# Two small products ahead of the attention-times-values step, another order of a turn's steps, and other PSUM banks

## The chip, the cores and the metric

The kernel runs on one core of one Trainium2 chip. The metric is device microseconds of one execution, lower is better. The profile names the engines PE (TensorE: matmul; PEld is its weight load), DVE (VectorE), ACT (ScalarE), POOL (GpSimd) and SP (SyncE, which here issues nearly all DMAs). All data is float32, apart from the attention mask and the identity that adds it.

## The reference

The input is x, 16 sequences of 256 tokens of 128 features. It is layer-normalised first. The result is `x + s * silu(f)`: `s` is one selective state-space block, `f` is a transformer of six layers, and both read the same normalised x.

```python
# s: the state-space block
xs, z = split(xn @ W_in)                       # 128 + 128 channels
xs, z = silu(conv4(xs)), silu(conv4(z))        # depthwise, 4 taps
dt_low, Bc, Cc = split(xs @ W_xdbl)            # 64, 16, 16
delta = softplus(dt_low @ W_dt + 2 * inv_dt)
h[n] = exp(-(n + 1) * delta) * h[n] + delta * xs * Bc[n]   # over 256 tokens, 16 states n
s = concat(sum_n h[n] * Cc[n] + xs * D, z) @ W_out + b_out

# f: six times
t = shift_tokens(f)                            # second half of the features moved by one token
q, k, v = split(t @ Wqkv)                      # 16 heads of 64
q, k = rotary(l2norm(q) * qs), rotary(l2norm(k) * ks)
# each window of 32 queries sees its own 32 keys and those of the window before
f = f + softmax(8 * q k^T + mask) v @ Wo
t = layernorm(shift_tokens(f)) * g + b
f = f + (a * gelu(gate)) @ W2 + b2             # a, gate = split(t @ W1 + b1), 341 each
```

## The kernel before

The work of the transformer is cut into blocks of 128 tokens: two blocks per sequence, 32 per layer, 192 in six layers. A program loop runs over turns n from -4 to 192. In each turn every step of the tuple `order` is called once, for a block that lies a fixed number ahead of n: `(project, 4, 0)` multiplies block n + 4 by the q weights, `(score, 1)` computes scores of block n + 1, `(attend, 0)` multiplies block n's weights by v. So five blocks are in work at once. The scheduler is set to manual, so the order in which the tuple calls the steps is the order in which each engine's queue holds the instructions; an engine runs its own queue strictly in that order, and engines wait for each other by semaphores.

What the steps issue, for one block (each file line is the one that the profile shows):

| Step | Engine and line | What |
|---|---|---|
| `project` (i = 0 q, 1 k), `values` | PE L427 | 128 tokens by 1024 columns, four passes of 512 columns |
| `square` | ACT L438 | squares for the lengths, read from PSUM |
| `rotate`, `rotate2` | DVE L448, L459 | the two rotary products, read from PSUM |
| `add` | POOL L470 | sum of the two rotary products |
| `hand_out` | ACT L480, SP L491 to L494 | v copied out of PSUM, then 8 or 10 DMAs that lay it out by window in `v2` |
| `lengths`, `guess` | DVE L504, L515 to L519 | sums of squares, first guess of the inverse roots for two blocks |
| `refine`, `scale` | POOL L525 to L535, L542 | two iterations on the guess; q or k times it |
| `turn` and `turned_q`, `turned_k` | PE L552, ACT L556 | eight transposes, then the copy out of PSUM |
| `score` | PE L587, L601 | mask by a product with the identity, then 64 small products |
| `greatest`, `subtract`, `soften` | DVE L614, L624, ACT L633 | maximum, subtraction, exponential |
| `turn_weights`, `turned_weights` | PE L552, ACT L556 | eight transposes of the weights, the copy into `aT` |
| `attend` | PE L657 | 64 products of 64 by 32 by 65 columns; the 65th column of v holds ones, so it gives the sum |
| `divide_last`, `divide` | DVE L673, ACT L674; DVE L680, L681 | division by that sum, last head pair apart |
| `turn_out`, `turned_out` | PE L552, ACT L556 | eight transposes of the output, the copy into `oT` |
| `close`, `residual` | PE L708, DVE L718 | output product for two blocks at a time (every second turn), sum with x |

Small shapes in `attend` and `score` use tiles of 64 rows by 32 columns of the array, eight at a time. Each fp32 product is two passes in the profile, so 64 products show as 128 matmuls.

Two other threads of work are woven in. `feed` advances a generator of the feed-forward part (PE L326, L181, L349, L372; ACT L330, L173, L338, L357; DVE L154, L155, L360, L375), one per four blocks, three steps a turn. The state-space block runs over eight groups of 512 tokens, 18 turns each, during about the first five of the six layers: `prepare` makes the inputs (convolution on DVE, L220 and L227, read from PSUM), and per turn `bring` (SP L270) loads one state's rows, `decay` (ACT L296) makes the exponential, `drive` (POOL L301) the input, `advance` (DVE L288) runs the scan instruction along the tokens, `weigh` (POOL L281, L282) adds the state's part to y; `put_out` ends a group. `norms_on` does the first layer normalisation of later groups in the early turns. In the last layer, `end` closes a group at the end of a turn (ACT L395 with silu, DVE L397, PE L401, DVE L402).

PSUM has eight banks of 512 float32 columns, held as one tensor. The dictionary `where` gives each role its bank; `pair(name)` takes two banks from there on, `bank(name)` one. Two roles in one bank can't be alive at once: a product that writes a bank waits until the last reader of the earlier contents is through. `at`, `aT`, `o`, `qT` are single buffers, `sq` and the scan's tensors have two, `bc` three.

Of the kernel before, what the change touches and what calls it, by code (L numbers as in the profile page):

```python
# [18 lines left out]
H, DH, W = 16, 64, 32  # L19
# [11 lines left out]
def tile_kernel(ctx: ExitStack, tc: tile.TileContext, a, out):  # L31
    nc = tc.nc
# [8 lines left out]
    pst = ctx.enter_context(tc.tile_pool(name="pst", bufs=1, space=PSUM))  # L41


    where = dict(q="6", k="0", v="4", qT="4", kT="0", s="2", w="4", av="2", o="2", h0="6", h1="0", h2="4", e="7", l="6", pw="4", f="7", n="1")
    psum = pst.tile([128, 8, G], FP, name="psum")

    def pair(name):
        i = int(where[name])
        return psum[:, i : i + 2, :].rearrange("p b x -> p (b x)")

    def bank(name):
        return psum[:, int(where[name]), :]
# [591 lines left out]
    def attend(n):  # L644

        b = blocks[n]
        aT, v2 = b["aT"], v2s[b["blk"]]

        b["pav"] = pair("av").rearrange("p (r x) -> p r x", r=2)[:, :, 0 : 7 * VW]
        b["pav"] = b["pav"].rearrange("p r (c d) -> p r c d", c=7)  # L650
        b["pav7"] = [bank("e"), bank("l")]
        for c in (7, 0, 1, 2, 3, 4, 5, 6):
            for j in range(4):
                jj = slice(j * W, (j + 1) * W)
                for r in range(2):
                    rr = slice(r * 64, (r + 1) * 64)
                    nc.tensor.matmul(  # L657
                        b["pav7"][r][jj, 0:VW] if c == 7 else b["pav"][jj, r, c, :],
                        aT[rr, c, jj],
                        v2[rr, j, c * VW : (c + 1) * VW],  # L660
                        start=True,
                        stop=True,
                    )
# [87 lines left out]
    def feed():  # L751
# [5 lines left out]


    order = (
        (norms_on, None),  # L760
        (lengths, 3, 1),
        (guess, 3),
        (close, -1, 1),
        (residual, -1),
        (feed, None),
        (project, 4, 0),
        (prepare, None),
        (score, 1),
        (rotate, 4, 0),
        (turn_weights, 0),  # L770
        (rotate2, 4, 0),
        (greatest, 1),
        (state, None, weigh),
        (refine, 3),
        (subtract, 1),
        (scale, 2, 0),
        (turned_weights, 0),
        (project, 4, 1),
        (square, 4, 0),
        (state, None, bring),  # L780
        (values, 1),
        (scale, 2, 1),
        (add, 4, 0),
        (rotate, 4, 1),
        (state, None, decay),
        (hand_out, 1),
        (rotate2, 4, 1),
        (add, 4, 1),
        (attend, 0),
        (divide_last, 0),  # L790
        (state, None, drive),
        (turn, 2, 0),
        (divide, 0),
        (state, None, advance),
        (square, 4, 1),
        (lengths, 4, 0),
        (turned_q, 2),
        (feed, None),
        (feed, None),
        (state, None, put_out),  # L800
        (turn_out, 0),
        (turned_out, 0),
        (turn, 2, 1),
        (turned_k, 2),
        (close, 0, 0),
        (soften, 1),
    )
    last = DEPTH * BL - 1
    with tc.manual_schedule():
# [124 lines left out]
```

## Time and profile before

| What | Value |
|---|---|
| Median of 3 runs | 3447.9 us (3443.46 to 3448.29) |
| Profiled execution | 3446.38 us, span 3444.6 us, mean granted TensorE clock 0.988 |
| Busy PE / PEld | 3238.9 us (94%) / 2163.4 us (63%) |
| Busy DVE / ACT / POOL | 2810.2 us (82%) / 2123.3 us (62%) / 2598.0 us (75%) |
| L427 q, k and v products on PE | 1070.3 us, 2304 passes, mean 600 ns |
| L657 attend on PE | 332.8 us, 24576 passes |
| L288 scan on DVE | 277.3 us, 128 instructions, mean 2166 ns |
| Copies of v, issued by SP | 1152 of 130 KB, 2.4 us from issue to landing; 576 of 65 KB, 2.5 us |

Times in the profile are microseconds unless marked ns. A row of the timeline reads: start, length, engine, line, operation, output from input with shapes, count, and in brackets the idle time just before with what ended it. Matmuls overlap in the array, so a group's busy time is longer than its start-to-start step; sums over a queue are made from steps. PE is 90% busy or more in nearly every fortieth of the span; only the first and the last are clearly below. The weight loads of PE run beside its products.

### The profile page before, as it was taken

What the parts mean: (1) busy time and instruction counts of PE and PEld (TensorE: products, weight loads), DVE (VectorE), ACT (ScalarE), POOL (GpSimd) and SP (SyncE); (2) the same over time, 40 slices, a digit from 0 to 9 for tenths busy, and PEclk for the clock granted to TensorE, in tenths of its full rate; (3) what the DMA queues carried; (4) which work ended last, traced back from release to release, by engine and by line L of the source; (5) the groups of instructions that cost most, each with busy time, mean ns of one, the idle gap of its engine ahead of it and who ended that gap; (6) DMA issues with size and microseconds to landing.
All of it is one profiled execution on the core that took longest, in us unless ns stands there. A gap on an engine that the chain in (4) does not pass through costs nothing.

```text
span 3444.6 us, 139812 instructions
## 1 busy us (share of the span) xinstructions
PE 3238.9 (94%) x62080; PEld 2163.4 (63%) x62080; DVE 2810.2 (82%) x3705; ACT 2123.3 (62%) x2725; POOL 2598.0 (75%) x2358
## 2 busy tenths in 40 slices
PE   6999999999999999999999999999999999999986
PEld 3666666666666666666666666666666666666663
DVE  6898879887898789878987889788879987777663
ACT  4666657655666566656665666576666665666554
POOL 6688868986898589968996789688878996565550
PEclk9999999999999999999999999999999999999998
DMA  3433334433333334333333333334333432222222
GB/s 87 104 98 105 84 84 104 104 81 83 97 97 90 91 94 97 91 85 88 107 92 91 88 96 92 89 99 98 91 81 93 105 94 70 69 64 70 63 64 57
DMA packets 190680, 304.49 MB, mean 88 GB/s; under 512 B 32702, under 2 KB 56572, under 8 KB 190076
## 3 DMA queue, kind: packets, MB, share of 16 engines
q1 hardware_dynamic: 189788, 295.22, 33.9%
q8 instruction: 488, 8.00, 1.0%
q14 instruction: 116, 0.95, 0.1%
q10 hardware_dynamic: 288, 0.33, 0.0%
HBM read 94.81 MB, written 8.91 MB: 30 GB/s over the span
## 4 chain that ended last, share of the span: by engine, by line
PE 73%; DVE 12%; ACT 6%; POOL 5%; issue 4%; DMA 0%; SPq 0%; DVEq 0%; ACTq 0%; POOLq 0%
PE psum L427 23%; PE psum L552 14%; PE psum L708 9%; PE psum L657 7%; PE psum L349 7%; PE psum L601 6%; PE psum L372 3%; ACT oT L556 3%; DVE t L459 2%; DVE o L681 2%; PE psum L587 2%; DVE hs L288 1%; DVE t L448 1%; POOL t L470 1%; DVE cv L227 1%
## 5 line engine op out<-in xcount | busy, mean ns | idle before, releaser
L470 POOL TENSOR_TENSOR t<-t,t 128x1024 f32<-128x1024 f32 x384 | 957.1, 2502 | 355.0 <-DVE t L459 184.4
L427 PE MATMUL psum<-wqkv,xT 128*128 128x512 f32 x2304 | 1070.3, 600 | 18.6 <-DVE cv L227 7.2
L542 POOL TENSOR_TENSOR t<-t,y 128x1024 f32<-128x1024 f32 x384 | 723.1, 1905 | 7.5
L427 PEld LDWEIGHTS psum<-wqkv,xT 128*128 128x128 f32 x2304 | 417.4, 192 | 406.0 <-issue 304.5
L448 DVE TENSOR_TENSOR t<-psum,tab 128x1024 f32<-128x1024 f32 x384 | 467.9, 1219 | 143.9 <-PE psum L427 131.1
L556 ACT COPY aT<-psum 128x1024 f32<-128x1024 f32 x192 | 194.2, 1012 | 589.6 <-PE psum L552 589.6
L459 DVE TENSOR_TENSOR t<-psum,tab 128x1024 f32<-128x1024 f32 x384 | 465.9, 1213 | 0.0
L504 DVE TENSOR_REDUCE ss<-sq 128x16 f32<-128x1024 f32 x384 | 456.4, 1198 | 1.3
L552 PE MATMUL psum<-ident,t 128*128 128x128 f32 x3072 | 412.7, 277 | 20.8 <-POOL t L542 8.9
L438 ACT ACTIVATE sq<-psum 128x1024 f32<-128x1024 f32 x384 | 395.0, 1029 | 51.4 <-DVE t L459 51.0
L657 PEld LDWEIGHTS psum<-v,aT 64*32 64x32 f32 x24576 | 294.0, 105 | 200.9 <-issue 121.9
L708 PE MATMUL psum<-oT,wo 128*128 128x256 f32 x1536 | 357.5, 386 | 24.2 <-ACT oT L556 24.2
L657 PE MATMUL psum<-v,aT 64*32 64x65 f32 x24576 | 332.8, 227 | 47.0 <-issue 24.6
L552 PEld LDWEIGHTS psum<-ident,t 128*128 128x128 f32 x3072 | 340.4, 142 | 40.3 <-POOL t L542 11.7
L708 PEld LDWEIGHTS psum<-oT,wo 128*128 128x128 f32 x1536 | 283.8, 190 | 81.4 <-ACT oT L556 46.5
L480 ACT COPY vt<-psum 128x1024 f32<-128x1024 f32 x192 | 196.2, 1022 | 189.6 <-PE psum L427 189.6
L601 PEld LDWEIGHTS psum<-kT,qT 64*32 64x32 f32 x24576 | 282.8, 105 | 11.2 <-issue 0.8
L601 PE MATMUL psum<-kT,qT 64*32 64x64 f32 x24576 | 286.2, 226 | 0.0
L288 DVE TENSOR_TENSOR_SCAN hs<-dA,bc 128x512 f32<-128x512 f32 x128 | 277.3, 2166 | 0.0
L556 ACT COPY oT<-psum 128x1024 f32<-128x1024 f32 x192 | 194.8, 1014 | 124.9 <-PE psum L552 123.0
L349 PE MATMUL psum<-xn,w 128*128 128x512 f32 (+1 forms) x576 | 260.2, 601 | 6.0 <-ACT o L674 4.8
L624 DVE TENSOR_TENSOR at<-psum,top 128x1024 f32<-128x1024 f32 x192 | 235.1, 1225 | 25.3
(102 smaller groups left out, 4583.0 us busy)
## 6 DMA issues: line engine op xcount, KB each, us to landing
v<-vt SPq DMA_DIRECT2D x1152, 130.0 KB, 2.4
bc<-rows SPq DMA_DIRECT2D x128, 512.0 KB, 5.1
v<-vt SPq DMA_DIRECT2D x576, 65.0 KB, 2.5
wqkv<-in_Wqkv SPq DMA_DIRECT2D x18, 512.0 KB, 4.0
wo<-in_Wo SPq DMA_DIRECT2D x6, 512.0 KB, 4.0
first<-in_x SPq DMA_DIRECT2D x8, 256.0 KB, 5.0
xn<-xT SPq DMA_DIRECT2D x16, 128.0 KB, 2.4
pad<-xn SPq DMA_DIRECT2D x8, 256.0 KB
```

The lines of the kernel that those rows point to most:

```text
L349: nc.tensor.matmul(ph[0:n, i * G : (i + 1) * G], w1[:, i * DI + c0 : i * DI + c0 + n], xn, start=True, stop=True,)
L427: nc.tensor.matmul(pq[:, cc], xb, wq[:, cc], start=True, stop=True)
L448: nc.vector.tensor_tensor(t1.rearrange("p (h d) -> p h d", h=H), b["pq", i].rearrange("p (h d) -> p h d", h=H), table(n, i, 0).unsqueeze(1 ...
L459: nc.vector.tensor_tensor(t2.rearrange("p (h f d) -> p h f d", h=H, f=2), b["pq", i].rearrange("p (h f d) -> p h f d", h=H, f=2)[:, :, ::- ...
L470: nc.gpsimd.tensor_tensor(b["qk", i], b["qk", i], b["t2", i], ALU.add)
L504: nc.vector.tensor_reduce(b["ss"][:, j * H : (j + 1) * H], b["sq", i].rearrange("p (h d) -> p h d", h=H), AX.X, ALU.add,)
L542: nc.gpsimd.tensor_tensor(t3, t3, b["inv"][:, j * H : (j + 1) * H].unsqueeze(2).to_broadcast([128, H, DH]), ALU.mult,)
L552: nc.tensor.transpose(pt[:, cc], of[:, cc], ident)
L556: nc.scalar.copy(to, pt.rearrange("p (c t) -> p c t", c=NP))
L601: nc.tensor.matmul(sc4[jj, r, c, :], qT[rr, c, jj], kT[rr, c, k0 : k0 + 64], start=False, stop=True, skip_group_check=True,)
L657: nc.tensor.matmul(b["pav7"][r][jj, 0:VW] if c == 7 else b["pav"][jj, r, c, :], aT[rr, c, jj], v2[rr, j, c * VW : (c + 1) * VW], start=Tru ...
L708: nc.tensor.matmul(b["pw"][:, 0:L], wo[:, c, :], b["oT"][:, c, :], start=(c == 0), stop=(c == NP - 1), skip_group_check=True,)
```

## The change

Three edits, shown whole below. In `attend`, two products of 32 by 4 columns (one for each half of the rows) are put ahead of the others. They read the first 32 columns of the last head pair's `aT` and one column of each of the four window pieces of `v2`, and write a corner of the two last-head banks, which the products after them write again. The table `where` gives most roles other banks; in particular the last head pair (`e`, `l`) moves to banks 3 and 2, which scores and v also use, and the roles n and f move. And `order` lists the same steps, each as often and for the same block as before, in another order. In short, by PE: before, a turn goes output product, q, scores, turned weights, k, v, attend, turned q, turned output, turned k; after, it goes output product, turned weights, scores, q, k, attend, v, turned output, turned k, turned q.

```diff
--- before.py
+++ after.py
@@ -41,7 +41,7 @@
     pst = ctx.enter_context(tc.tile_pool(name="pst", bufs=1, space=PSUM))
 
 
-    where = dict(q="6", k="0", v="4", qT="4", kT="0", s="2", w="4", av="2", o="2", h0="6", h1="0", h2="4", e="7", l="6", pw="4", f="7", n="1")
+    where = dict(q="6", k="0", v="2", qT="6", kT="2", s="2", w="0", av="4", o="4", h0="6", h1="4", h2="0", e="3", l="2", pw="4", f="6", n="5")
     psum = pst.tile([128, 8, G], FP, name="psum")
 
     def pair(name):
@@ -649,6 +649,12 @@
         b["pav"] = pair("av").rearrange("p (r x) -> p r x", r=2)[:, :, 0 : 7 * VW]
         b["pav"] = b["pav"].rearrange("p r (c d) -> p r c d", c=7)
         b["pav7"] = [bank("e"), bank("l")]
+
+        for r in range(2):
+            rr = slice(r * 64, (r + 1) * 64)
+            nc.tensor.matmul(
+                b["pav7"][r][0:W, 0:4], aT[rr, 7, 0:W], v2[rr, :, 0], start=True, stop=True
+            )
         for c in (7, 0, 1, 2, 3, 4, 5, 6):
             for j in range(4):
                 jj = slice(j * W, (j + 1) * W)
@@ -757,53 +763,53 @@
 
 
     order = (
-        (norms_on, None),
+        (close, -1, 1),
         (lengths, 3, 1),
+        (state, None, advance),
         (guess, 3),
-        (close, -1, 1),
         (residual, -1),
+        (turn_weights, 0),
+        (state, None, decay),
+        (prepare, None),
+        (turned_weights, 0),
         (feed, None),
-        (project, 4, 0),
-        (prepare, None),
-        (score, 1),
-        (rotate, 4, 0),
-        (turn_weights, 0),
-        (rotate2, 4, 0),
-        (greatest, 1),
         (state, None, weigh),
         (refine, 3),
+        (state, None, put_out),
+        (norms_on, None),
+        (score, 1),
+        (scale, 2, 1),
+        (greatest, 1),
+        (project, 4, 0),
+        (project, 4, 1),
         (subtract, 1),
+        (attend, 0),
+        (soften, 1),
+        (rotate, 4, 0),
+        (divide_last, 0),
+        (rotate2, 4, 0),
+        (values, 1),
+        (square, 4, 1),
+        (divide, 0),
         (scale, 2, 0),
-        (turned_weights, 0),
-        (project, 4, 1),
+        (state, None, drive),
+        (rotate, 4, 1),
+        (state, None, bring),
         (square, 4, 0),
-        (state, None, bring),
-        (values, 1),
-        (scale, 2, 1),
+        (rotate2, 4, 1),
         (add, 4, 0),
-        (rotate, 4, 1),
-        (state, None, decay),
         (hand_out, 1),
-        (rotate2, 4, 1),
+        (feed, None),
         (add, 4, 1),
-        (attend, 0),
-        (divide_last, 0),
-        (state, None, drive),
-        (turn, 2, 0),
-        (divide, 0),
-        (state, None, advance),
-        (square, 4, 1),
-        (lengths, 4, 0),
-        (turned_q, 2),
         (feed, None),
-        (feed, None),
-        (state, None, put_out),
         (turn_out, 0),
         (turned_out, 0),
         (turn, 2, 1),
         (turned_k, 2),
+        (turn, 2, 0),
+        (turned_q, 2),
         (close, 0, 0),
-        (soften, 1),
+        (lengths, 4, 0),
     )
     last = DEPTH * BL - 1
     with tc.manual_schedule():
```

## The prediction

> **What bounds the kernel now.** I read the page's busy times first, then the TensorE queue in order of time through a quiet stretch (four turns, half of them with the scan's light work beside it), then VectorE and SyncE in the same stretch.
>
> ```profile
> PE 3238.9 (94%) x62080; PEld 2163.4 (63%) x62080; DVE 2810.2 (82%) x3705; ACT 2123.3 (62%) x2725; POOL 2598.0 (75%) x2358
> PE 73%; DVE 12%; ACT 6%; POOL 5%; issue 4%; DMA 0%; SPq 0%; DVEq 0%; ACTq 0%; POOLq 0%
> ```
>
> TensorE is busy for 94% and carries 73% of the chain. The change adds almost no product, so only TensorE's waits can be won: one must see how large they are, and where.
>
> ```profile
> 1665.79 3.72 PE L708 MATMUL psum<-oT,wo 128*128 128x256 f32 x16 [0.23 <-ACT oT L556]
> 1669.35 1.88 PE L427 MATMUL psum<-wqkv,xT 128*128 128x512 f32 x4
> 1671.16 0.41 PE L587 MATMUL psum<-mask,ident_h 64*32 64x512 bf16 x8
> 1671.39 1.46 PE L601 MATMUL psum<-kT,qT 64*32 64x64 f32 x128
> 1672.78 1.09 PE L552 MATMUL psum<-ident,at 128*128 128x128 f32 x8
> 1673.71 3.60 PE L427 MATMUL psum<-wqkv,xT 128*128 128x512 f32 x8
> 1677.23 1.70 PE L657 MATMUL psum<-v,aT 64*32 64x65 f32 x128
> 1678.86 1.09 PE L552 MATMUL psum<-ident,t 128*128 128x128 f32 x8
> 1679.79 2.74 PE L372 MATMUL psum<-u,w 128*128 128x512 f32 x6
> 1682.37 1.04 PE L552 MATMUL psum<-ident,o 128*128 128x128 f32 x8
> 1683.24 1.04 PE L552 MATMUL psum<-ident,t 128*128 128x128 f32 x8
> 1684.12 2.08 PE L427 MATMUL psum<-wqkv,xT 128*128 128x512 f32 x4
> ...
> 508.64 0.45 PE L657 MATMUL psum<-v,aT 64*32 64x65 f32 x16 [0.54 <-ACT sq L438]
> 510.02 1.39 PE L657 MATMUL psum<-v,aT 64*32 64x65 f32 x112 [0.93 <-DVE at L624]
> ...
> 3290.12 1.12 PE L401 MATMUL psum<-ident,xn 128*128 128x128 f32 x4 [5.42 <-DVE xn L397]
> 3291.03 3.48 PE L427 MATMUL psum<-wqkv,xT 128*128 128x512 f32 x4
> ```
>
> Start to start, a turn costs TensorE: q 1.81, masks and scores 1.62, turned weights 0.93, k and v 3.52, attend 1.63, turned q 0.93, turned output 0.87, turned k 0.88: 12.19 us. Each second turn adds the output product, 3.56. Four turns add one feed-forward: two sets of four transposes at 0.68, the wide products 5.26, the narrow ones 2.58, together 9.20. Four turns thus need 4 x 12.19 + 7.12 + 9.20 = 65.1 us. The starts of L708 give two turns 31.6 and 35.1 in quiet places: 66.7. So a quiet four has only 1.6 us of waits, mostly 0.23 before each output product and about 0.4 before the wide products. But from the first L708 (92.98) to the 80th (2831.49) are 79 steps of two turns in 2738.5 us, 69.3 per four: 104 us above the quiet rate, of which the scan's own products (about 5.7 us in each of 8 groups) are some 46 and new norms a few. Some 54 us are waits in disturbed turns, such as the two rows at 508 and 510: the scan's convolution (L220, L227, 3.1 us of VectorE) has pushed the subtraction back. After 2831 the eight closing pieces stop TensorE for 5.42 us each.
>
> VectorE and SyncE:
>
> ```profile
> L288 DVE TENSOR_TENSOR_SCAN hs<-dA,bc x128: 1212/2086/3366, 158.7 to 2846.0; 128x512 f32<-128x512 f32 x128
> 1712.82 0.59 SPq L491 DMA_DIRECT2D v<-vt  x1
> 1713.46 1.68 SPq L492 DMA_DIRECT2D v<-vt  x1
> 1715.18 1.87 SPq L494 DMA_DIRECT2D v<-vt  x3
> ```
>
> The scan instruction takes 1.2 to 3.4 us. SyncE needs some 6.7 us to issue one block's copies of v (1710.32 to 1717.05), and each lands 2.4 us (median) after its issue.
>
> **The change, part by part.** Write A for the start of attend on TensorE, S for the moment VectorE is through with the subtraction (A is never before S, as banks 2 and 3 now also take the last head pair).
>
> *Small products.* Two of them, two passes each: four more passes a turn. Row first: 128 passes of attend take 1.63 us, 12.7 ns each, so 0.05 us a turn, 10 us in 192 turns. [...] The bounds are nothing, if they hide in a wait, and 0.43 us a turn if two pairs run end to end at the 0.217 us that one pass lasts, 83 us. I take 10: eight tiles of this shape overlap in the row beside it. They also collect all waits for v at the front of attend.
>
> *TensorE's order* becomes: output product, turned weights, scores, q, k, attend, v, feed-forward, turned output, turned k, turned q. Sum per four turns: 65.1 + 0.2 = 65.3. The walk:
> - Attend needs S. From S, VectorE does q's rotations and three reciprocals with the division (3.7 us, the division not before attend's end at A + 1.9), k's rotations (done by A + 5.5), two lengths 2.2, scan 2.1, every second turn guess and residual 1.4, maximum and subtraction 2.5: 12.8, or 14.2. TensorE's turns are 12.2 or 15.8 before feed-forward. The feed-forward gives each light turn something: 0.68 in one, 2.58 in the other (VectorE then 1.5 more), so 12.9 and 14.8 against VectorE's 12.8 and 14.3. VectorE keeps about 0.5 to 0.85 us of lead, as scores end 3.5 us before attend and maximum plus subtraction take 2.5.
> - v overwrites the last heads' banks, read by ScalarE at S + 1.9; attend ends at A + 1.7. Free while the lead is over 0.3, else up to 0.4.
> - Turned output waits for the division (A + 3.2; TensorE is there at A + 3.4): free. Turned k waits for v's copy (ScalarE, A + 4.6; there at A + 5.0 or later): free. The 0.23 before the output product goes, as turned k and q now lie between.
> - New: scores of the next turn need q turned at the very end of this one. From the turned output's start T, ScalarE ends its three evictions at T + 3.95, TensorE reaches the scores at T + 3.6. With an output product (3.56) between it is covered; in the two light turns it costs 0.4 to 0.5 each.
> Intervals of attend by this walk: 16.45, 13.35, 21.0, 15.2: 66.0; a long scan in the light turns adds about 0.2. 66.2 against 66.7: 0.5 x 48 = 24 us won.
>
> *Moved queues.* POOL: both scales now follow refine directly; they end 2.5 us or more before their transposes by the rows' durations (2.37, 1.90, refine 3.9 start to start), so nothing. SyncE: `bring` lies behind `weigh`, early on POOL, and no longer in front of a waiting copy. v's copies start at A + 4.6 instead of just before attend; last landing by the rows at A + 12.0 to 13.6, attend at A + 13.35 in the tightest turn. Cover is nearly gone there. Ends: nothing, and 1 us in each of 48 such turns, 48 us; I take 8.
>
> *Banks.* The scan's preparation gets bank 5, away from k (0, 1): k no longer waits for the convolution. The convolution still precedes the subtraction on VectorE: in a light turn 3.1 us less lead and the added 0.95 of TensorE, about 1.3 us, where before lost 2.0 to 2.5; in a heavy turn nearly nothing. I halve the 54 us: 25 won. Ends: nothing, and 54.
>
> *Closing pieces.* The row before shows 5.42 us idle, and then 3.48 for a q product that takes 1.88. [...] In the new order silu follows the last eviction; table load 1.28, two silu 1.26, product 0.69 give about 4.65. [...] Filling and draining: 5, since k in the fill waits 3.8 and 3.4 us for the convolution's bank.
>
> Sum, against the profiled execution (3446.4 with 3444.6 of span, 1.5 below the median): -24 - 25 - 6 - 5 + 8 = -52, so 3394.
>
> **The rivals.**
> 1. *VectorE becomes the bound in light turns* (slower). Place: scores to attend, where only 3.5 us of q and k cover 2.5 us of VectorE; before it was 4.45 us, with turned weights between. Price: each us that VectorE is late delays attend by one, then v by up to 0.4, in 96 light turns. It decides above 12.9 us of VectorE between subtractions; it is at 12.8 by rows. For it: the scan reaches 3.4 instead of 2.1. Against: POOL waits for guess in every second turn, leaving it free. If it holds at 1 us, 96 us lost minus part of the gains: 3480. Break-even is about 0.55 us a light turn.
> 2. *The order gains nothing*: new waits (scores, v) make up for the old ones, 66.7 per four, and the convolution hurts as before: 3447, within 10.
> 3. *More is won*: no waits at the scores or v and none left of the 54: 3446 - 48 x 0.9 - 54 - 11 = 3338.
>
> **Numbers.** My forecast 0.55; rival 1 0.25; rival 2 0.12; rival 3 0.08. Range 3345 to 3465: it takes in the small products' upper part, late v, and half of rival 1. The forecast's own range is 3365 to 3425. 0.2% (7 us) is about what a measurement here can tell. Faster: 0.55 + 0.08 + half of rival 2's 0.12 = 0.69. Same 0.06, slower 0.25.
>
> **What would show it.** Right: two-turn steps sum to about 66 in quiet places; no wait before L708; 0.3 to 0.5 before L587 or L601 in light turns, ended by ACT qT; cv turns lose 1 us or so; a closing gap near 4.6. Rival 1: attend waits for DVE at L624 in most light turns, v for ACT o. Late copies: waits at the small products with no engine named. Wrong: quiet fours over 66.7, or a group of the small products that costs over 0.3 us.

## The result, and the profile after

| | Before | After |
|---|---|---|
| Median | 3448.1 us (3443.46 to 3451.16) | 3525.64 us (3522.62 to 3542.41) |
| Ratio after/before, 95% interval | | 1.0241 [1.022, 1.0261] |
| Profiled execution: time, span, mean clock | 3446.38, 3444.6, 0.988 | 3542.41, 3540.6, 0.970 |

The change makes the kernel 2.4% slower; 3394 us was forecast, and the range ended at 3465. The profiled execution after is 17 us above its median, so what follows are shares of 96 us (3540.6 - 3444.6), not of 78. In the changed file the small products are L655, attend L663, the output product L714.

First the instruction queue on the page of before, then the page of the kernel after: busy times, chain, instruction queue, and three groups of products (busy time, mean ns of one, idle time ahead with what ended it).

```profile
q8 instruction: 488, 8.00, 1.0%
```

```profile
PE 3286.1 (93%) x62848; PEld 2200.0 (62%) x62848; DVE 2755.6 (78%) x3705; ACT 2110.1 (60%) x2725; POOL 2567.3 (73%) x2358
PE 83%; DVE 6%; issue 5%; POOL 2%; ACT 2%; DMA 1%; SPq 1%; ACTq 0%; POOLq 0%; DVEq 0%
q8 instruction: 495, 8.11, 1.0%
L427 PE MATMUL psum<-wqkv,xT 128*128 128x512 f32 x2304 | 1130.2, 628 | 18.8 <-ACT sq L438 8.0
L663 PE MATMUL psum<-v,aT 64*32 64x65 f32 x24576 | 319.9, 229 | 93.8 <-issue 93.8
L655 PE MATMUL psum<-v,aT 64*32 64x4 f32 x768 | 51.3, 178 | 39.9 <-DVE at L624 27.4 <-DMA v<-vt 12.3
```

VectorE, ScalarE and GpSimd are all less busy than before, by share and in us, which speaks against one of them as the new bound. TensorE's share of the chain rose from 73% to 83%. "issue" means that the engine waited for nothing that the profile shows, and attend now carries 93.8 us of it. The same wide products of q, k and v take 628 ns instead of 600. The clock is part of it: 94 passes touch stretches of half clock, 30 before. Of the 28 ns, 15 are left where the clock was full (610 against 595).

TensorE's waits (us in total, times, longest), three of before and then five of after:

```profile
PE psum L657 <- issue: 24.6, 21, 3.0
PE psum L708 <- ACT oT L556: 24.2, 94, 1.1
PE psum L657 <- DVE at L624: 14.4, 15, 1.1
```

```profile
PE psum L663 <- issue: 93.8, 48, 4.9
PE psum L401 <- DVE xn L397: 43.7, 8, 7.1
PE psum L655 <- DVE at L624: 27.4, 18, 2.7
PE psum L655 <- DMA v<-vt: 12.3, 11, 3.1
PE psum L601 <- ACT qT L556: 5.9, 35, 0.3
```

One term grows by 69 us: pauses of attend with no engine named. They lie in its middle, not at its start. TensorE's timeline shows where the forecast holds and where it breaks:

```profile
2092.59 3.62 PE L714 MATMUL psum<-oT,wo 128*128 128x256 f32 x16
...
2126.86 3.62 PE L714 MATMUL psum<-oT,wo 128*128 128x256 f32 x16
...
2158.26 3.62 PE L714 MATMUL psum<-oT,wo 128*128 128x256 f32 x16
...
1748.31 1.72 PE L601 MATMUL psum<-kT,qT 64*32 64x64 f32 x128 [0.16 <-ACT qT L556]
1749.96 3.70 PE L427 MATMUL psum<-wqkv,xT 128*128 128x512 f32 x8
1753.60 0.20 PE L655 MATMUL psum<-v,aT 64*32 64x4 f32 x2
...
1753.66 1.46 PE L663 MATMUL psum<-v,aT 64*32 64x65 f32 x114
1756.72 0.32 PE L663 MATMUL psum<-v,aT 64*32 64x65 f32 x9 [1.60 <-issue]
1756.97 1.98 PE L427 MATMUL psum<-wqkv,xT 128*128 128x512 f32 x4
...
1331.60 1.30 PE L663 MATMUL psum<-v,aT 64*32 64x65 f32 x99
1337.84 0.66 PE L663 MATMUL psum<-v,aT 64*32 64x65 f32 x24 [4.94 <-issue]
1338.43 3.78 PE L427 MATMUL psum<-wqkv,xT 128*128 128x512 f32 x4
1342.00 5.86 PE L349 MATMUL psum<-xn,w 128*128 128x512 f32 x12
```

The output products at 2092.59, 2126.86 and 2158.26 are 34.3 and 31.4 apart: 65.7 for a quiet four turns, 66.7 before, 66.2 forecast. There is no wait ahead of them. But few fours are so quiet: up to the 80th output product the median four takes 67.7 us, 66.9 before. Then two pauses: after most of attend's products have run, the same queue of the same products stops for 1.60 or 4.94 us. All its operands were there, since the passes around it read the same tiles. After the long pause v's product takes 3.78 us instead of 1.98.

The clock's row for the same place (us, PE, PEld, DVE, ACT and POOL busy with instructions, granted clock, DMA share, GB/s):

```profile
1332.00:1338.00 6.00, 1.06 (x93) 0.90 (x90) 1.35 (x3) 2.34 (x4) 6.00 (x5) 0.86 0.48 87
1338.00:1342.00 4.00, 4.00 (x29) 1.76 (x23) 3.35 (x4) 0.00 (x0) 1.35 (x1) 0.50 0.02 4
1342.00:1346.00 4.00, 4.00 (x10) 1.77 (x9) 0.95 (x2) 2.99 (x3) 3.58 (x2) 0.86 0.29 61
1346.00:1352.00 6.00, 6.00 (x37) 4.56 (x36) 4.18 (x6) 4.51 (x6) 1.26 (x1) 1.00 0.70 185
```

The pause costs more than its length: 4.94 us idle, then 4 us at a clock of 0.50 and 4 us at 0.86, which lose another 2.6. Over the whole execution, the time lost to the clock (each piece of time by one minus its granted clock) is 106.5 us after and 43.8 before, 63 more. Of these, 48 fall into time in which products ran (77 against 29); the rest falls into pauses and costs nothing of its own. So of the 96 us, the clock has 48 and the pauses without a named engine 71 (38.2 to 109.2 over all lines); waits for VectorE (13) and for v (12) come on top, the wait for the output's copy (-23) goes off. The remainder, some -25, is quicker turns and smaller waits, and is not split here.

**What ends the pauses.** The queue that the page names "q8 instruction" carried 495 packets of 16,384 bytes after and 488 before. TensorE's records, weight loads and semaphore instructions included, number 126,864 after and 124,979 before; divided by 256 that is 495.6 and 488.2. In all fourteen traces the number of packets (486 to 496) is that of the records by 256, rounded down. So one packet is 256 of TensorE's instructions, 64 bytes each. A turn has 256 in attend and 272 in the scores, and runs through them at four every 25 ns. I numbered TensorE's records and looked at every step of more than 0.5 us inside attend:

```
                        steps over 0.5 us    of them at place 193 of each 256
                        number   us          number   us
before                  34        45.9       19        28.3
after                   54       114.9       48       104.3
```

After, 48 of 54 resume at the same place in the count of 256 (give or take two), and all of those between 1.15 and 1.57 us after the end of an instruction packet. Numbered in order, packets and places pair up over the whole execution: at none of the 494 places did TensorE go on earlier than 1.14 us after the end of its packet. For the 4.94 us pause, on the profile's axis: TensorE passed that place last in the scores at 1327.66; the rows load of 512 KB was issued at 1330.78, behind nine copies of v; the next instruction packet started on the DMA engines only at 1335.42 and ended at 1336.38; TensorE went on at 1337.84. In half of all cases the next packet starts 0.6 to 1.3 us after the place is passed; it takes about 1 us. So it matters how much later it starts, and how long TensorE takes to the next such place. Where one place falls into the scores and the next into attend:

```
          cases   to the next place (median us,    packet starts more       pauses us
                  the pause not counted)           than 3 us late
before    168     5.89                             21                        3.9
after     182     5.01                             33                       54.1
```

Every pause in this table came with a packet that started more than 3 us late. Both parts got worse: there are more late packets, and 0.9 us less of other work covers each. A load of the scan's rows issued near the place (from 3 us ahead to 1 us behind) goes with later starts, 2.42 against 1.16 us in the mean before and 2.25 against 1.58 after; but after, 40.1 of the 54.1 us of pauses stand in the cases without one. So the rows alone are not the cause.

SyncE's queue ahead of the 4.94 us pause:

```profile
1325.49 1.29 SPq L491 DMA_DIRECT2D v<-vt  x1
1326.84 0.58 SPq L492 DMA_DIRECT2D v<-vt  x1
1327.46 1.87 SPq L494 DMA_DIRECT2D v<-vt  x3
1330.78 0.38 SPq L270 DMA_DIRECT2D bc<-rows  x1
```

Attend uses up its 256 or 264 instructions in 1.5 to 1.6 us, while a packet's start (1.0 us behind the place in the median), its length (1.0) and the time from its end until TensorE goes on (1.15 us or more) come to 3 us or more, 10.2 us in the case above. The new order also brings scores and attend closer: between their starts lay 6.07 us (scores 1.62, turned weights 0.93, k and v 3.52), now lie about 5.2 (scores, q and k).

### The profile page after: what moved, and what is told of

The parts are those of the page before. It is cut to its first block, busy times and chain, and to the rows that moved or that the text cites. A ratio compares the mean times of both kernels' runs of the same rounds, so it can differ in the third digit from the quotient of the medians.

```text
span 3540.6 us, 141644 instructions
## 1 busy us (share of the span) xinstructions
PE 3286.1 (93%) x62848; PEld 2200.0 (62%) x62848; DVE 2755.6 (78%) x3705; ACT 2110.1 (60%) x2725; POOL 2567.3 (73%) x2358
## 3 DMA queue, kind: packets, MB, share of 16 engines
q1 hardware_dynamic: 189788, 295.22, 32.4%
## 4 chain that ended last, share of the span: by engine, by line
PE 83%; DVE 6%; issue 5%; POOL 2%; ACT 2%; DMA 1%; SPq 1%; ACTq 0%; POOLq 0%; DVEq 0%
PE psum L427 27%; PE psum L552 17%; PE psum L714 9%; PE psum L663 7%; PE psum L349 7%; PE psum L601 7%; PE psum L372 3%; PE psum L587 1%; PE psum L655 1%; DMA v<-vt 1%; DVE at L624 1%; DVE top L614 1%; DVE ss L504 1%; DVE cv L227 1%; PE psum L181 1%
## 5 line engine op out<-in xcount | busy, mean ns | idle before, releaser
L470 POOL TENSOR_TENSOR t<-t,t 128x1024 f32<-128x1024 f32 x384 | 923.8, 2413 | 522.9 <-DVE t L459 314.6
L427 PE MATMUL psum<-wqkv,xT 128*128 128x512 f32 x2304 | 1130.2, 628 | 18.8 <-ACT sq L438 8.0
L542 POOL TENSOR_TENSOR t<-t,y 128x1024 f32<-128x1024 f32 x384 | 736.9, 1940 | 7.1
L633 ACT ACTIVATE at<-at 128x1024 f32<-128x1024 f32 x192 | 203.0, 1057 | 529.3 <-DVE at L624 529.2
L663 PE MATMUL psum<-v,aT 64*32 64x65 f32 x24576 | 319.9, 229 | 93.8 <-issue 93.8
L614 DVE TENSOR_REDUCE top<-psum 128x16 f32<-128x1024 f32 x192 | 234.7, 1222 | 217.8 <-PE psum L601 194.4
L552 PE MATMUL psum<-ident,t 128*128 128x128 f32 x3072 | 380.3, 275 | 13.8 <-POOL t L542 7.1
L438 ACT ACTIVATE sq<-psum 128x1024 f32<-128x1024 f32 x384 | 371.9, 1028 | 15.3 <-PE psum L427 9.8
L714 PE MATMUL psum<-oT,wo 128*128 128x256 f32 x1536 | 347.5, 379 | 1.1 <-ACT oT L556 1.1
L663 PEld LDWEIGHTS psum<-v,aT 64*32 64x32 f32 x24576 | 278.3, 106 | 102.7 <-issue 101.8
L601 PE MATMUL psum<-kT,qT 64*32 64x64 f32 x24576 | 300.0, 226 | 15.4 <-issue 8.8
L714 PEld LDWEIGHTS psum<-oT,wo 128*128 128x128 f32 x1536 | 284.3, 190 | 36.0 <-ACT oT L556 1.3
```

The costliest lines, as they stand in the source:

```text
L427: nc.tensor.matmul(pq[:, cc], xb, wq[:, cc], start=True, stop=True)
L470: nc.gpsimd.tensor_tensor(b["qk", i], b["qk", i], b["t2", i], ALU.add)
L542: nc.gpsimd.tensor_tensor(t3, t3, b["inv"][:, j * H : (j + 1) * H].unsqueeze(2).to_broadcast([128, H, DH]), ALU.mult,)
L552: nc.tensor.transpose(pt[:, cc], of[:, cc], ident)
L601: nc.tensor.matmul(sc4[jj, r, c, :], qT[rr, c, jj], kT[rr, c, k0 : k0 + 64], start=False, stop=True, skip_group_check=True,)
L663: nc.tensor.matmul(b["pav7"][r][jj, 0:VW] if c == 7 else b["pav"][jj, r, c, :], aT[rr, c, jj], v2[rr, j, c * VW : (c + 1) * VW], start=Tru ...
```

## The experiments

Summary first; all ratios are to the kernel before, timed beside each. "Attend pauses" are attend's waits with no engine named, in the profiled execution.

| Kernel | Median us | Ratio [95%] | Attend pauses us (times) | Lost to clock us |
|---|---|---|---|---|
| after | 3525.64 | 1.0241 [1.022, 1.0261] | 93.8 (48) | 106.5 |
| e1 rows load later | 3545.64 | 1.0277 [1.0255, 1.03] | 61.7 (37) | 106.8 |
| e2 no small products | 3472.56 | 1.0068 [1.0041, 1.0096] | 64.6 (40) | 74.4 |
| e3 small products alone | 3463.51 | 1.0044 [1.0024, 1.0065] | 53.3 (44) | 58.9 |
| e4 rows not loaded | 3483.93 | 1.0112 [1.0086, 1.0138] | 59.8 (38) | 86.3 |
| e5 e2 without v's copies | 3372.24 | 0.9788 [0.9764, 0.9812] | 10.7 (12) | 64.4 |
| e6 after, no copies or rows | 3360.93 | 0.975 [0.9735, 0.9764] | 0.8 (1) | 52.5 |
| e7 before, no copies or rows | 3378.77 | 0.9803 [0.9787, 0.982] | none | 42.2 |
| e8 small, one piece | 3512.49 | 1.0187 [1.0154, 1.022] | 71.7 (43) | 88.1 |
| e9 e2, weights turned later | 3520.36 | 1.0202 [1.0169, 1.0234] | 37.1 (31) | 72.6 |
| e10 before, weights turned earlier | 3509.04 | 1.0172 [1.0155, 1.019] | 24.9 (25) | 43.8 |
| e11 before, rows in two loads | 3431.6 | 0.9953 [0.9938, 0.9967] | 16.1 (20) | 45.7 |
| e12 e2, rows in two loads | 3458.86 | 1.003 [1.0015, 1.0045] | 41.9 (28) | 67.7 |

**The two parts apart.** e2 takes the small products out of the changed kernel; e3 puts them alone into the kernel before.

```diff
-        for r in range(2):
-            rr = slice(r * 64, (r + 1) * 64)
-            nc.tensor.matmul(
-                b["pav7"][r][0:W, 0:4], aT[rr, 7, 0:W], v2[rr, :, 0], start=True, stop=True
-            )
```

> The changed kernel without the two small products, order and banks as changed. Theory 1: 8 of some 660 TensorE instructions a turn go, so fetches are needed 1.2% less often and 10 us of passes go: 3500 to 3520. Theory 2: 3515. Theory 3: back to about 3440 or below.

> The kernel before with the two small products and nothing else of the change. Theory 1: 10 us of passes and a little more waiting for instructions, 3450 to 3470. Theory 2: 3458. Theory 3: 3500 or more.

Measured: 3472.56 and 3463.51. The order and the banks alone lose 24 us, the small products alone 15, both together 78. So the small products cost 53 us in the new order, though their own group is busy for only 0.27 us a turn and mostly overlapped. The parts don't add. In both e2 and e3 the row that moves most is attend's pauses: 64.6 and 53.3 us against 24.6 before.

**What the small products wait for.** e8 lets them read four columns of one window piece in place of one column of all four, so that they collect the waits of one piece only.

```diff
-                ... aT[rr, 7, 0:W], v2[rr, :, 0], start=True, stop=True
+                ... aT[rr, 7, 0:W], v2[rr, 0, 0:4], start=True, stop=True
```

> The changed kernel, but the two small products read four columns of the first window piece of v instead of one column of each of the four: as many passes and instructions, but no longer a front where all copies are waited for. If the extra instructions are what the small products cost (attend with them is 264 TensorE instructions, more than one fetch of 256): 3515 to 3530, as with them. If the collected waits are: 3465 to 3485, as without them.

Measured 3512.49, 13 us less than after, with the waits for v down from 12.3 to 3.8 us (and two new waits of the small products without a named engine, 5.4 us). The single executions of the two just overlap, so about a quarter of the 53 us, at most, is the collecting of waits. The rest comes with the instructions: eight for the small products (two products of two passes and their weight loads) and in the kernel after three more semaphore instructions a turn (1168 such records of TensorE, 591 in e2 and in e8). With them attend is more than 256 instructions, and two ends of a packet can fall into one attend. That was seen 10 times after (18.7 us of pauses), 9 times in e3 (12.9), 2 times before (0.6) and once in e2 (0). How the rest of the 53 us divides is not shown.

Their own time can be read where nothing disturbs: from the first product of attend to the next group, in e2, after, e7 and e6 (the last two are described below; they lack the copies of v):

```profile
1705.57 1.70 PE L658 MATMUL psum<-v,aT 64*32 64x65 f32 x128
1707.20 1.98 PE L427 MATMUL psum<-wqkv,xT 128*128 128x512 f32 x4
...
3016.92 0.20 PE L655 MATMUL psum<-v,aT 64*32 64x4 f32 x2
...
3018.45 1.98 PE L427 MATMUL psum<-wqkv,xT 128*128 128x512 f32 x4
...
1711.36 1.54 PE L659 MATMUL psum<-v,aT 64*32 64x65 f32 x128
1712.83 1.09 PE L554 MATMUL psum<-ident,t 128*128 128x128 f32 x8
...
1700.68 0.20 PE L657 MATMUL psum<-v,aT 64*32 64x4 f32 x2
...
1702.21 1.98 PE L429 MATMUL psum<-wqkv,xT 128*128 128x512 f32 x4
```

Without copies, attend takes 1.47 us without the small products and 1.53 with them: 0.06 us a turn, 12 us in 192. With copies it takes 1.63 without them and from 1.53 with them (the median turn after is 1.59): the small products then shorten attend, as the waits for v no longer stand between its products, where they stretch some eight steps to 36 ns or more instead of mostly 17. So the 53 us are not their work on the array.

**Moving the rows load.** e1 puts `weigh`, behind which `bring` stands, later in the turn, to keep the 512 KB away from attend's packet.

```diff
-        (state, None, weigh),
         (refine, 3),
 ...
         (scale, 2, 0),
+        (state, None, weigh),
         (state, None, drive),
```

> The changed kernel with one edit: weigh (two POOL products of the scan) comes after the second scale instead of before refine. Its product is what the next load of the scan's rows (bring, 512 KB) waits for, so the load is issued around the start of attend or a little later, and no longer in the 3 to 6 us ahead of it. Theory 1 (TensorE runs out of instructions in attend: its fetches of 16 KB queue on the DMA engines behind the scan's rows and the copies of v, which the new order has moved right ahead of attend): TensorE's idle time inside attend that no engine ends falls from 93.8 us to about 40, the clock recovers with it, time 3525 down to 3430 to 3470. Theory 2 (VectorE is the bound between scores and attend): no change beyond 10 us. Theory 3 (the small products themselves cost it): no change.

Measured 3545.64, where 3430 to 3470 was expected: slower still. Attend's pauses fell to 61.7 us, but the scores now had 32.2 and the small products waited 25.5 us for v. The transfer was moved in front of another packet and of the copies. That agrees with the collision and speaks against this place as the cure; it proves neither.

**Taking the transfers away.** e4 loads the rows three times in all and uses the three buffers again. e5 takes e2 and lays out v for the first blocks only. e6 (the changed kernel, small products included) and e7 (the kernel before) leave out both.

```diff
+            bc[n + 2] = kept[(n + 2) % 3]
+            if g == 0 and n + 2 < 3:                  # e4, e6, e7: the load
 ...
-        for r in range(2):
+        for r in range(2) if n < 2 else ():           # e5, e6, e7: hand_out
```

> The changed kernel in which the scan's rows are loaded only for the first three states of the first group; three kept tensors are used again and again for all other states (the computation of the scan's values is left out in that sense; every product stays). 125 of 128 loads of 512 KB are gone. Theory 1: the waits for instructions inside attend fall from 93.8 us to 30 or less (the copies of v remain), time 3400 to 3440. Theory 2: VectorE and POOL do the same work, 3525. Theory 3: 3525.

> The changed order and banks without the small products, and without the copies of v by window after the first two blocks (what attend reads is stale; every product stays). Without that edit it took 3472.6 us. Theory 1 (TensorE's instruction fetches wait on the DMA engines behind these copies and the scan's rows): idle time of TensorE that no engine ends falls from 75 us to 20 or less, lost clock from 74 to about 55: 3395 to 3415. Theory 2 (the order's own waits between engines): 3465 to 3475, only the few us of late v go.

> The changed kernel, small products kept, with neither the copies of v after the first two blocks nor the scan's rows after the first three states (stale values; every product stays). Theory 1: nearly no waits for instructions remain, and the queue walk of the prediction holds: 3380 to 3405. Theory 2: 3470 or more. Theory 3 (the small products cost time by themselves): 3430 or more.

> The kernel before with the same two kinds of DMA left out. Theory 1: it loses its 38 us of waits for instructions and some of its lost clock: 3395 to 3415, so that with the DMAs gone the changed order is even with it or ahead. Theory 2: 3440 to 3450, and the changed order stays behind it by 20 us or more.

Without the rows, 3483.93: 42 us less than after but far from the 3400 to 3440 expected, with 59.8 us of attend's pauses left. Without the copies, 3372.24, 100 us below e2, with attend's pauses at 10.7: the copies of v are the larger part of the collision. Without both, the page of e6 and its attend group:

```profile
q1 hardware_dynamic: 37228, 39.87, 4.1%
q8 instruction: 492, 8.06, 1.0%
L665 PE MATMUL psum<-v,aT 64*32 64x65 f32 x24576 | 305.7, 228 | 0.8 <-issue 0.8
```

The data queue moved 295 MB before and after; here it moves 40. TensorE's instructions come in nearly as many packets as ever (492) and attend loses 0.8 us, once, where it lost 93.8. And the changed kernel (3360.93) is now faster than the kernel before without the same transfers (3378.77), by 18 us. This splits the 96 us of the profiled spans:

```
                       without copies and rows   with them   their price
before                 3376.9                    3444.6       67.7
after                  3359.8                    3540.6      180.8
after minus before      -17.1                      96.0      113.1
```

The price by TensorE's groups (each product's start to the next one's start): attend 118 us after and 54 before, q, k and v 22 and -7, scores about 23 and 4. A caution: a copy that isn't issued also spares its waits. In e2 the waits for v that the profile names were only 3.8 us of the 100 that e5 won; but undisturbed attend takes 1.63 us in e2 and 1.47 in e5, some 30 us of the 100 in 192 turns. The same 30 us are in the 67.7 of before. After they are mostly gone already, so the price of the collision alone probably rose by more than 113 us. The packets agree: between scores and attend none starts more than 3 us late in e6 or e7.

**More room between the bursts.** e9 takes e2 and turns the weights between scores and attend again, as before the change. e10 goes the other way in the kernel before: weights turned ahead of the scores.

```diff
         (score, 1),
+        (turn_weights, 0),
+        (turned_weights, 0),                          # e9, from e2
```

```diff
+        (turn_weights, 0),
         (score, 1),
         (rotate, 4, 0),
-        (turn_weights, 0),                            # e10, from before
```

> The changed order and banks without the small products (3472.6 us), with turned weights moved from ahead of the scores to between scores and q: again 4.45 instead of 3.5 us of products with few instructions lie between the two groups of 256. Theory 1 (a fetch that starts in the scores must be there before attend has used up its instructions): idle time in attend that no engine ends falls from 64.6 us to 35 or less. The price is that scores now follow the last eviction of q by 0.9 us less, in 96 light turns: waits for ACT qT rise from about 5 to 60 us or more. Time 3470 to 3510. Theory 2 (spacing doesn't matter, only the amount of DMA does): waits in attend stay at 60 or more, time 3520 or more.

> The kernel before with one step moved: turned weights come ahead of the scores, so that attend follows the scores by 3.5 us of k and v instead of 4.45. No DMA is added, and the copies of v stay where they were. Theory 1: waits in attend that no engine ends rise from 24.6 to 40 to 60 us and lost clock by 10 or more, 3470 to 3490. Theory 2: they stay, and the time with them, at 3445 to 3455.

Half of this worked. In e9 attend's pauses fell from 64.6 to 37.1 us: from a place in the scores to the next in attend are 5.90 us now (5.15 in e2), and late packets there leave 22.0 us of pauses in 24 cases (45.3 in 30). But 3520.36 is 48 us slower than e2, as the scores now come earlier than their inputs:

```profile
PE psum L601 <- ACT qT L556: 42.8, 82, 0.6
PE psum L658 <- issue: 37.1, 31, 3.7
PE psum L587 <- ACT kT L556: 17.8, 39, 0.5
```

In e10 attend's pauses stayed at 24.9 in sum. Those with a place in the scores before them did rise, from 3.9 to 18.7 us, with 5.14 us to the next place; others fell. New are 22.2 us without a named engine at the scores and 29.6 us that turned weights wait for the exponential. Its 61 us are thus not those of the change, and the clock did not fall. The distance from scores to attend matters in both; that it alone explains the change is not shown.

**Smaller transfers.** If the packet is late behind 512 KB, halves with a part of the queue between them should help. e11 does it in the kernel before, e12 in e2.

```diff
-                out=bc[n + 2], in_=of[g]["rows"][:, n + 2, :].partition_broadcast(128)
+                out=bc[n + 2][:, 0, :], in_=of[g]["rows"][0, n + 2, :].partition_broadcast(128)
 ...
         (hand_out, 1),
+        (state, None, bring_c),                       # loads the second half
```

> The kernel before, but each load of the scan's rows of 512 KB is cut into two of 256 KB: the input's half where the load was, the output's half behind the copies of v. If the length of one load is what holds up a fetch, waits for instructions fall from 38 to 20 us and the time to 3420 to 3440; if the bytes alone count, no change, and SyncE's further issue may cost a few us: 3445 to 3460.

> The changed order and banks without the small products (3472.6 us), with the scan's rows loaded in two halves of 256 KB, the input's half where the load was and the output's half behind the copies of v, as in the kernel before with that edit (3431.6 us). Theory 1, long loads in front of a fetch: 3440 to 3460. But here the next input's half follows the output's half at once, since nothing holds SyncE between them, so the two may act as one load: then 3465 to 3480. Theory 2: no change, 3472.

Measured: e11 3431.6, e12 3458.86 (14 less than e2). e11 beats both kernels, by 0.5% and 2.7%. Its packets that start over 3 us late between scores and attend fell from 21 to 9 (in e12 to 18, from 30 in e2), as the theory of long loads has it. Its pauses in attend fell by 8.5 us of the 16 won; the other half I can't place. The new order stays behind before even with halves.

## Why the prediction was wrong, point by point

The step that failed is the term for the moved queues. It put v's copies at 8 us, for the cases in which they land late, and put at nothing what copies and rows do to other traffic on the way. The runs show that the transfers cost 181 us after and 68 before, 113 more, 64 of them in attend, where TensorE waits for its own instructions.

- **TensorE's walk, 66.2 per quiet four.** Right, if anything a little high: 65.7 where nothing collides, and no wait ahead of the output product (24.2 us in 94 waits before, 1.1 us after). The scores wait 0.16 us in light turns, not 0.4 to 0.5. With the transfers away the whole change is worth -17 to -18 us; the forecast had -24 for this term.
- **v's copies, 8 us; the failing step.** Right for what it asked: waits of 12.3 us with 11 late landings. It asked only when the copies land, and not what else they hold up; no term of the sum had room for that. The view was there: `issue` stood with 24.6 us in 21 waits at attend in the waits of before, and q8 in the table of queues.
- **Small products, 10 us.** Right as work of the array: 0.06 us a turn, 12 us in 192 turns, where nothing else changes. Their price, 53 us in the new order and 15 in the old, is in the bounds that the prediction gave (0 to 83), but by luck: "four more passes a turn" were costed as work of the array, while they are also eight more instructions in a stream that was already short at that place.
- **The convolution's 54 us, halved.** The 54 us were a remainder, and the convolution was named for them without a count. The waits of before name 14.4 us of attend for the subtraction, 6.6 for the squares and 7.2 of k for the convolution; another 38.2 us in the same trace have no named engine and belong to the failing step. After, attend no longer waits for the squares and k no longer for the convolution, but the waits for the subtraction rose to 27.4, up to 2.7 each; the walk's light turns were too tight. With the transfers away it is still 29.5 against 17.2 plus 7.1 for the squares, so there is no gain where 25 was forecast.
- **Closing pieces, 4.65 us a gap.** 4.1 in e6 (32.9 in 8), against 4.8 in e7: the mechanism holds when the transfers are away. With them it is 5.5 after and 5.0 before, one of 7.12. No run of the change as it is shows the 6 us that the sum has for these pieces; they were the author's estimate. With the transfers the eight gaps grew by 4.0 us (39.7 to 43.7 in all), without them they shrank by 5.6 (38.5 to 32.9).
- **Filling and draining, 5 us.** 2.2 by the profile: the first output product starts 3.6 us earlier, and from the last one to the end it takes 1.4 us longer.
- **The clock.** The sum has no term for it, though the time lost to it rose by 63 us. After the first 60 us of the kernel after, half clock set in during a pause of TensorE or within 1.5 us behind it at 30 of 39 pauses over 1.9 us, and at 1 of 37 between 1.0 and 1.9. Of attend's 48 pauses without a named engine 18 were over 1.9 us. By the longest pause ahead of each stretch of half clock, the 63 us divide into 36 for those pauses, 12 for waits for the subtraction, 10 for the closing gaps and 7 for v.
- **Rival 1 (VectorE the bound)** is a small part: 13 us more of waiting for the subtraction, in 18 waits and not in most light turns, and the 12 us of clock. **Rivals 2 and 3** are refuted. The slower side was given 0.25, and none of it for the mechanism that decided.

What stays open: why a packet of instructions starts up to 7.8 us after the place is passed between scores and attend (11.0 elsewhere) when copies and rows are in flight. Which DMA engine carries it, and what stands in front of it there, the records don't show; that it shares a way with the data is concluded from the runs without the transfers. The new banks were never run without the new order, so what each of them does is open too.

## What to carry to other kernels

Count instructions as well as time on an engine that runs bursts of tiny products: where 256 of them pass faster than a packet arrives (here about 3 us, and up to 10 with transfers in front), more instructions and transfers issued at that moment can delay the engine. Take waits whose releaser is "issue" in the middle of a group of like products for a sign of such a delay, number the instructions to confirm it, and confirm the cause by taking the transfers away. An order that is faster on a quiet machine (17 us here) can lose several times that (113 us) by moving bursts and transfers together.

## What was not expected of the hardware

- TensorE's instructions came in packets of 16,384 bytes, one for each 256 instructions. Packets were late though the mean data rate was only 86 GB/s and the data queue's share 32.4%; with the data queue at 40 MB instead of 295, attend lost 0.8 us to them. TensorE resumed 1.15 to 1.57 us after a packet's end.
- The small products cost 0.28 us a turn in the new order (53 us in 192 turns), where their own steps take 0.06.
- Four passes more at the front of attend, which take up the waits for v, shorten an undisturbed attend from 1.63 to 1.53 us (e2 and the kernel after).
- Half clock set in at 30 of the 39 pauses over 1.9 us in the kernel after, counted from its 60th us on, and at 1 of 37 between 1.0 and 1.9: 43.8 us lost to the clock before, 106.5 after.
